# Loading the adjacency matrix in two halves from ScalarE's queue, and turning it by halves, in a two-layer graph network on one core

## The chip, the cores and the metric

The kernel runs on one core of one Trainium2 chip. The metric is the device time of one execution in microseconds; three executions of the kernel before gave 1511.56, 1512.70 and 1513.59, median 1512.7 us. A lower number is better.

## What is computed

The input `x` has 32 graphs of 512 nodes with 128 features, all in fp32, and `adj` is one 512 x 512 matrix shared by all. The reference, cut to what matters:

```python
# layer 0: graph convolution of order 3; both adjacencies are the same adj
parts = [x[..., None], chebyshev(adj, x), chebyshev(adj, x)]      # adj x, adj^2 x, adj^3 x, twice
x = layernorm(x + einsum('bnik,iok->bno', concat(parts, 3), weight_1))
# layer 1: five gated steps, then the residual
h = x
for _ in range(5):
    m = einsum('nm,bmd->bnd', adj, h); av = concat([m, m], -1)    # in and out matrix are both adj
    u = h @ u3.T + u3_b
    z = sigmoid(av @ w3.T + w3_b + u)
    r = sigmoid(av @ w4.T + w4_b + u)
    hv = tanh(av @ w5.T + w5_b + (r * h) @ u5.T + u5_b)
    h = (1 - z) * h + z * hv
x = layernorm(x + h)
```

Since the adjacency is the same throughout, the kernel adds the two halves of each layer-1 weight, and the weights of equal powers in layer 0. It computes layer 0 with the square of adj, which it forms once.

## The kernel before, in words

**Tiles and stages.** The 32 graphs go through as 16 pairs. `pair(q, key0)` describes one pair: `layer0`, then five steps, each made of a product of adj with both graphs' state (`pair_product`) and, for each graph, the gates (`gates`). The state is needed in two layouts: features on the partitions (`hT`) for the gates, nodes on the partitions (`X`) for the product with adj. Each step therefore ends with a turn of `hT` into `X`. From pair 2 on, layer 0 works on two pairs at once for the products with adj (`quad_product`).

**Products in seven.** Every product of 2 x 2 blocks is done with seven block products in place of eight (`seven`, line 393). The sums of blocks that this needs are made beforehand: `T` (four sums of adj's blocks, by VectorE, line 234), `TT` (the same one level down, line 249), `at2S` (sums of the square's blocks, line 496), and sums of the state's blocks `S` by POOL (line 511). In `seven`, products one, three, five and six go into one PSUM bank and are read out between by a copy on ScalarE (line 385) or an add on VectorE (lines 386, 389). Product three can't begin before the copy of product one, and so on.

**Turns.** By DMA, a turn is `turn` (line 345): VectorE turns 32 x 32 blocks into a buffer `v` (line 360), SP writes it to DRAM in four transfers and fetches it back in another order. There are five buffers `v`; layer 0 also takes two of them for its result (`vy`, line 857) and, for each turned input, one more as a landing place. By TensorE, a turn is four transposes (`transposes`, line 299) and a copy by ScalarE. `ON_PE = {14: 2, 15: 2}` (line 23) says how many last steps of which pair use TensorE (line 1073). Where the last step is among them, the end of the pair is not a turn either: `finish` (line 1010; `last_finish`, line 977, for the last pair) adds the residual and the turned state by products with the identity in PSUM, 4 + 4 for each graph (line 1018), and norms from there. Other pairs turn by DMA, add on POOL (line 1113) and norm from SBUF.

**The order of the work.** `Plan` (line 47) writes the order out by hand. Each operation has an engine, a cost in us, a key, the operations that it comes after, and the buffers that it takes and gives; `late` is how long after its issue a result counts as there (for a DMA, its latency). `run` (line 75) goes through time with these numbers and emits, on each free engine, the ready operation with the smallest key. The engines then execute exactly that order, each waiting on semaphores where something isn't there. `KEYS` (line 24) is the start key of each pair, `SQ_KEY` that of the square of adj, `TT_KEY` that of the sums `TT`.

**The opening.** SP issues the two graphs of pair 0 (`first_x`, line 218), then four transfers of a quarter of adj each (`load_adj`, line 213: blocks 11, 21, 12, 22; 256 KB each, 1 KB pieces), then layer 0's weight `w0` (line 257). ScalarE loads its table, and copies. TensorE turns pair 0's x (line 302), multiplies adj's blocks with x (line 524), and turns adj itself (`transposes` at line 434, four banks of four turns) for the left side of its square. ScalarE copies the four banks (`an`, line 437), VectorE sums their blocks (line 453), and the seven products of the square follow (line 460). The two graphs of pair 1 are loaded from ScalarE's queue (`second_x`, line 206), those of later pairs from SP's. `w0` is summed on VectorE into `wc` and `wt` (lines 261 to 267), the weights of layer 0's channel products (line 766).

The line that the new argument of the sums `T` replaces is 235; the waits of the pair's products on adj's blocks are at lines 550 and 551:

```python
T_sums.append(plan("DVE", 0.69, emit, after=at_in + T_sums[:2], key=-50.0))
...
(L[0], lambda: B11, [f11, in11]),
(L[1], lambda: B21, [f12, in21]),
```

Of the kernel before, what the change touches and what calls it, by code (L numbers as in the profile page):

```python
# [17 lines left out]
H = NK // 2  # L18
HN = N // 2
R = 32  # L20
NR = P // R
STEPS = 5
ON_PE = {14: 2, 15: 2}
KEYS = [-2.0, 20.0, 50.0, 68.0, 92.0, 118.0, 154.0, 168.0, 186.0, 214.0, 234.0, 268.0, 294.0, 322.0, 346.0, 358.0]
LONG = 19.0
TT_KEY = 45.0
SQ_KEY = 10.0
KEPT = 3
FIRST = 2
SINGLE = 2  # L30
# [96 lines left out]
def gnn_resnorm_kernel(  # L127
# [17 lines left out]
    nc = tc.nc  # L145
# [8 lines left out]
    def tiles(tag, n, shape=(P, N), pool=work):  # L154
        return [pool.tile(list(shape), F32, tag=f"{tag}_{i}", name=f"{tag}_{i}") for i in range(n)]

    slots = dict(
        bank=tiles("bank", 8, pool=psum),
# [7 lines left out]
        UY=tiles("UY", 2, (P, 4, N)),  # L166
        h0=tiles("h0", 4, (P, 2, NK, P)),
# [4 lines left out]
        z=tiles("z", 3),  # L172
        m=tiles("m", 5),
        S=tiles("S", 2, (P, 7, H, P)),
        v=tiles("v", 5),
        two=[None] * 5,
        inside=[None] * 17,
    )
    plan = Plan(slots)

    def chunk(k):
        return slice(k * P, (k + 1) * P)


    at = const.tile([P, NK, N], F32, tag="at", name="at")
    ident = const.tile([P, P], F32, tag="ident", name="ident")
# [23 lines left out]
        first = plan("ACT", 0.45, lambda: emit(0), after=after, key=-60.0, late=3.2)  # L210
        return first, plan("ACT", 0.45, lambda: emit(1), after=after, key=-60.0, late=3.2)

    def load_adj(i, j, key):
        k, c = slice(i * H, (i + 1) * H), slice(j * HN, (j + 1) * HN)
        emit = lambda: nc.sync.dma_start(at[:, k, c], adjT[:, k, c])
        return plan("SP", 0.46, emit, key=key, late=4.0)

    def first_x():
        emit = lambda: load_x(0, 0)
        a = plan("SP", 0.42, emit, take=[("xg", "xg0")], key=-99.0, late=2.9)  # L220
        b = plan("SP", 0.42, lambda: load_x(0, 1), key=-98.0, late=3.4)
        return a, b

    x_in = {0: first_x()}
    in11, in21 = load_adj(0, 0, -95.0), load_adj(1, 0, -94.0)
    at_in = [in11, in21, load_adj(0, 1, -90.0), load_adj(1, 1, -90.0)]

    B11, B12 = at[:, :H, :HN], at[:, :H, HN:]  # L230
    B21, B22 = at[:, H:, :HN], at[:, H:, HN:]
    T_sums = []
    for i, (a, b) in enumerate(((B12, B11), (B22, T[:, 0]), (B22, B12), (B21, T[:, 1]))):
        emit = lambda i=i, a=a, b=b: nc.vector.tensor_tensor(T[:, i], a, b, ALU.subtract)
        T_sums.append(plan("DVE", 0.69, emit, after=at_in + T_sums[:2], key=-50.0))


    TT_sums = []
    for i, n, of in (
# [8 lines left out]
        for j, (a, b) in enumerate(((b12, b11), (b22, t(0)), (b22, b12), (b21, t(1)))):  # L248
            emit = lambda d=t(j), a=a, b=b: nc.vector.tensor_tensor(d, a, b, ALU.subtract)
            after = T_sums + own[:2]  # L250
            own.append(plan("DVE", {4: 0.7, 2: 0.85, 1: 0.28}[n], emit, after=after, key=TT_KEY))
        TT_sums += own
# [1 line left out]


    w_of = lambda: plan["w0"].rearrange("p k f -> p (k f)")[:, : 7 * P]
    w0_in = plan("SP", 0.45, lambda: nc.sync.dma_start(w_of(), w0), take=[("UY", "w0")], key=-70.0, late=7.0)

    def layer0_weights():
        w_raw = w_of().rearrange("p (o k) -> p o k", k=7)  # L260
# [38 lines left out]
    def transposes(dst, src_of):  # L299

        for k in range(NK):
            nc.tensor.transpose(dst[:, chunk(k)], src_of(k), ident)  # L302
# [76 lines left out]
    def into(dst, cols, plus=None):  # L379

        def first(i, j):
            if plus is None:
                return "ACT", COPY[cols], lambda src: nc.scalar.copy(dst(i, j), src)  # L385
            return "DVE", ADD[cols], lambda src: nc.vector.tensor_tensor(dst(i, j), src, plus(i, j), ALU.add)

        def second(i, j):
            return "DVE", ADD[cols], lambda src: nc.vector.tensor_tensor(dst(i, j), src, dst(i, j), ALU.add)  # L389

        return first, second
# [39 lines left out]
    an_of = lambda km: plan[f"an{km // H}"].rearrange("p b k c -> p (b k c)").rearrange("p (k n) -> p k n", k=H)  # L431
    an_ready = []
    for km in range(NK):
        emit = lambda km=km: transposes(plan[f"ba{km}"], lambda k: at[:, k, chunk(km)])
        take = [("bank", f"ba{km}")] + ([("h0", f"an{km // H}")] if km % H == 0 else [])
        tr = plan("PE", 0.44, emit, after=at_in, take=take, key=SQ_KEY)
        emit = lambda km=km: nc.scalar.copy(an_of(km)[:, km % H], plan[f"ba{km}"])
        an_ready.append(plan("ACT", 0.59, emit, after=[tr], give=[("bank", f"ba{km}")], key=SQ_KEY))

    an_block = lambda i, l: lambda: an_of(l * H)[:, :, i * HN : (i + 1) * HN]  # L440
    an_sum = lambda i: lambda: plan[f"anS{i // H}"][:, i % H].rearrange("p k c -> p (k c)").rearrange(
# [3 lines left out]
    for i, (a, b, op) in enumerate(  # L445
# [7 lines left out]
        emit = lambda i=i, a=a, b=b, op=op: nc.vector.tensor_tensor(an_sum(i)(), a(), b(), op)  # L453
        take = [("h0", f"anS{i // H}")] if i % H == 0 else []
        sums.append(plan("DVE", 0.69, emit, after=an_ready + sums[-2:], take=take, key=SQ_KEY))

# [24 lines left out]
    give = [("h0", f"{t}{i}") for t in ("an", "anS") for i in range(2)]  # L481
    _, squared = seven("sq", an_ready, 1.72, terms, square_product, into(dst, N), SQ_KEY + 1, whole, give=give)

# [4 lines left out]
    for i, (a, b, op) in enumerate(  # L488
# [7 lines left out]
        emit = lambda i=i, a=a, b=b, op=op: nc.vector.tensor_tensor(at2S[:, i], a, b, op)  # L496
        A2_sums.append(plan("DVE", 0.69, emit, after=squared + A2_sums[-2:], key=SQ_KEY + 1))

    half_bank = lambda bank: bank[:, :HN]

    def copied(dst, src, turned, engine, after, key):

        to = nc.scalar.copy if engine == "ACT" else nc.gpsimd.tensor_copy
        emit = lambda: to(fit(dst(), turned), src())  # L504
        return plan(engine, 0.41 if engine == "ACT" else 0.4, emit, after=after, key=key)

    def fit(t, turned):
        return t.rearrange("p k (s d) -> p k s d", d=R) if turned else t

    def add(us, dst, a, b, op, after, key):  # L510
        emit = lambda: nc.gpsimd.tensor_tensor(dst(), a(), b(), op)  # L511
        return plan("POOL", us, emit, after=after, key=key)

    def pair_product(X_of, turned, name, dst, S, slots, after, key):

        X11, X12, X21, X22 = [
            lambda b=b, h=h: X_of(b)[:, h * H : (h + 1) * H] for b in range(2) for h in range(2)
        ]  # L520

        def product(dst, left, right, first, last):
            for k in range(H):
                nc.tensor.matmul(  # L524
                    dst,
                    lhsT=left[:, k, :],
                    rhs=right[:, k, :],
                    start=(first and k == 0),
                    stop=(last and k == H - 1),
                    skip_group_check=True,  # L530
                )

        own = plan("-", 0.0, lambda: None, after=list(after[0]), take=slots, key=key)
        both = list(after[1]) + [own]
        S_of = lambda i: lambda: S(i)
        F = lambda i: lambda: fit(S(i), turned)
        if turned:
            f11 = copied(S_of(4), X11, True, "ACT", [own], key)
            f12 = copied(S_of(5), X12, True, "ACT", [f11], key)
        else:  # L540
            f11 = f12 = own
        s0 = add(0.73, F(0), X21, X22, ALU.add, both, key)
        s1 = add(0.73, F(1), F(0), X11, ALU.subtract, [s0], key)
        s2 = add(0.73, F(2), X11, X21, ALU.subtract, both, key)
        s3 = add(0.73, F(3), X12, F(1), ALU.subtract, [s1], key)
        f22 = copied(S_of(6), X22, True, "POOL", both, key) if turned else own
        L = (S_of(4), S_of(5), S_of(6)) if turned else (X11, X12, X22)
        t = lambda i: lambda: T[:, i]
        terms = [
            (L[0], lambda: B11, [f11, in11]),  # L550
            (L[1], lambda: B21, [f12, in21]),
            (S_of(1), t(1), [s1, T_sums[1]]),
            (S_of(0), t(0), [s0, T_sums[0]]),
            (S_of(2), t(2), [s2, T_sums[2]]),
            (L[2], t(3), [f22, T_sums[3]] + both),
            (S_of(3), lambda: B22, [s3]),
        ]
        give = [o for o in slots if o[0] == "S"]
        p, (e11, e12, e21, e22) = seven(
            name, [f11], 0.86, terms, product, into(dst, HN), key, half_bank, give=give  # L560
        )
        read = [s0, s1, s2, s3, f11, f12, f22] if turned else p + [s2, s3]
        return [[e11, e12], [e21, e22]], [read] * 2
# [471 lines left out]
    def pair(q, key0):  # L1035
# [6 lines left out]
        for s in range(STEPS):  # L1042
# [27 lines left out]
            if s > 0:  # L1070
                for b in range(2):
                    plan("-", 0.0, lambda: None, after=read[b], give=[("X", f"X{q}_{s - 1}_{b}")], key=key)
            by_dma = s < STEPS - ON_PE.get(q, 0)

# [54 lines left out]
    for q in range(NP):  # L1129
        pair(q, KEYS[q])  # L1130
    with tc.manual_schedule(engines=None):
# [54 lines left out]
```

## Time and profile before

| What | Value |
|---|---|
| median of three executions | 1512.7 us |
| the profiled execution, its own time | 1512.07 us |
| its span, first to last instruction | 1510.3 us |
| TensorE busy | 1493.2 us, 99% of the span |
| VectorE, POOL, ScalarE busy | 1024.4, 848.7, 750.7 us |
| adj's four transfers, issue to landing | 5.0 to 5.6 us |
| pair 0's x, first half, issue and first use | 0.72 and 3.69 us |
| w0, issue and landing | 3.63 us and 6.1 us later |

The profile is of one execution. "PE" is TensorE's matmul, "PEld" its weight load, DVE VectorE, ACT ScalarE, POOL GpSimd; an engine's name with q is its sequencer, which issues DMAs. A list of instructions in order of time shows start and length in us, engine, line, operation, output and input tiles with their shape, the count, and in brackets the idle time before it with what ended it. A matmul's length includes its drain, so following matmuls overlap. The chain of work goes back from the last instruction to what released each one. A list of waits shows who waited for whom: total us, times, longest.

### The profile page before, as it was taken

The numbers are of one execution on the slowest core, as the hardware profiler recorded it, in microseconds if no ns is written. First come the engines' busy times: TensorE is split into PE (matmuls) and PEld (weight loads), VectorE is DVE, ScalarE is ACT, GpSimd is POOL, SyncE is SP. The second block draws the span as 40 slices with busy tenths as digits, with TensorE's granted clock in tenths as the row PEclk, the third lists the DMA queues.
The fourth block names the chain that finished last, engine by engine and source line by source line (L and its number), as shares of the span: only waits on it lengthen the run. The fifth ranks groups of instructions, "written<-read, shape, count | busy, mean of one in ns | idle before, by whom it ended". The sixth has DMA issues, their size and how long they took to land.

```text
span 1510.3 us, 21064 instructions
## 1 busy us (share of the span) xinstructions
PE 1493.2 (99%) x6562; PEld 1042.3 (69%) x6562; DVE 1024.4 (68%) x2125; ACT 750.7 (50%) x1584; POOL 848.7 (56%) x1207
## 2 busy tenths in 40 slices
PE   8999999999999999999999999999999999999997
PEld 7877777676667776677676766676766776666665
DVE  6566666767776758667767567768477666766665
ACT  3454444654644644455445445546444455545454
POOL 4856834764544947756367455558464644543454
PEclk9999999999999999999999999999999999999998
DMA  3114423333333433334243242534333332433310
GB/s 110 57 56 112 107 75 92 110 107 84 105 103 107 126 98 93 107 95 119 71 139 90 77 120 92 133 98 126 81 109 92 90 84 70 119 86 89 77 50 28
DMA packets 166176, 142.91 MB, mean 95 GB/s; under 512 B 18992, under 2 KB 128048, under 8 KB 166064
## 3 DMA queue, kind: packets, MB, share of 16 engines
q1 hardware_dynamic: 165776, 141.04, 33.9%
q8 instruction: 52, 0.85, 0.3%
q14 instruction: 60, 0.49, 0.1%
q10 hardware_dynamic: 288, 0.52, 0.1%
HBM read 71.76 MB, written 69.73 MB: 94 GB/s over the span
## 4 chain that ended last, share of the span: by engine, by line
PE 94%; DVE 2%; POOL 1%; issue 1%; DMA 1%; SPq 0%; ACT 0%; POOLq 0%; DVEq 0%
PE bank L909 35%; PE bank L524 32%; PE bank L1049 9%; PE bank L766 6%; PE bank L831 6%; PE bank L628 4%; PE bank L460 1%; PE bank L302 0%; POOL rstd L320 0%; POOL S L511 0%; DVE M L685 0%; DMA at<-in_adjT 0%; DVE UY L685 0%; PE bank L1018 0%; DMA X<-d 0%
## 5 line engine op out<-in xcount | busy, mean ns | idle before, releaser
L974 POOL TENSOR_TENSOR hT<-z,hT 128x512 f32<-128x512 f32 x156 | 199.0, 1281 | 303.9 <-DVE z L972 297.9
L524 PE MATMUL bank<-T,S 128*128 128x256 f32 x1232 | 307.0, 379 | 0.2 <-POOL S L511 0.2
L524 PEld LDWEIGHTS bank<-T,S 128*128 128x128 f32 x1232 | 229.1, 190 | 78.2 <-ACT m L385 28.9
L385 ACT COPY m<-bank 128x256 f32<-128x256 f32 x320 | 119.1, 372 | 277.6 <-PE bank L524 276.5
L524 PE MATMUL bank<-at,S 128*128 128x256 f32 x824 | 211.4, 379 | 0.9 <-ACT S L504 0.6
L389 DVE TENSOR_TENSOR m<-bank,m 128x256 f32<-128x256 f32 x240 | 100.3, 419 | 137.0 <-PE bank L524 94.7
L524 PEld LDWEIGHTS bank<-at,S 128*128 128x128 f32 x824 | 153.7, 190 | 57.3 <-issue 37.3
L970 DVE TENSOR_TENSOR bank<-bank,hT 128x512 f32<-128x512 f32 x156 | 107.8, 694 | 104.4 <-ACT bank L956 103.6
L909 PE MATMUL bank<-rh,u5s 128*128 128x512 f32 (+1 forms) x324 | 159.3, 587 | 0.2 <-ACT bank L936 0.2
L1049 PE MATMUL bank<-hT,u3s 128*128 128x512 f32 x320 | 159.3, 592 | 0.0
L909 PE MATMUL bank<-m,w4s 128*128 128x512 f32 x320 | 158.6, 592 | 0.0
L909 PE MATMUL bank<-m,w3s 128*128 128x512 f32 x320 | 157.0, 592 | 0.0
L909 PE MATMUL bank<-m,w5s 128*128 128x512 f32 x320 | 155.1, 593 | 0.2 <-DVE M L389 0.2
L917 ACT ACTIVATE bank<-bank 128x512 f32<-128x512 f32 x160 | 93.2, 583 | 121.1 <-DVE bank L915 120.7
L1054 ACT ACTIVATE uT<-bank,ub3s 128x512 f32<-128x512 f32 x160 | 109.7, 687 | 83.9 <-PE bank L1049 82.7
L915 DVE SCALAR_TENSOR_TENSOR bank<-bank,b4s,uT 128x512 f32<-128x512 f32 x160 | 119.6, 750 | 46.3 <-PE bank L909 44.1
L956 ACT ACTIVATE bank<-bank,hv_b 128x512 f32<-128x512 f32 x158 | 104.3, 662 | 77.1 <-PE bank L909 76.0
L922 DVE SCALAR_TENSOR_TENSOR bank<-bank,b3s,uT 128x512 f32<-128x512 f32 x160 | 118.9, 750 | 13.8 <-PE bank L909 13.1
L924 ACT ACTIVATE z<-bank 128x512 f32<-128x512 f32 x160 | 95.1, 595 | 59.9 <-DVE bank L922 55.7
L360 DVE STREAM_TRANSPOSE v<-hT 128x512 f32<-128x512 f32 x152 | 105.5, 699 | 20.0 <-POOL hT L974 19.4
L918 DVE TENSOR_TENSOR rh<-bank,hT 128x512 f32<-128x512 f32 x160 | 107.8, 679 | 10.0 <-ACT bank L917 9.2
L972 DVE TENSOR_TENSOR z<-bank,z 128x512 f32<-128x512 f32 x156 | 105.1, 682 | 1.6
(182 smaller groups left out, 2456.1 us busy)
## 6 DMA issues: line engine op xcount, KB each, us to landing
d<-v SPq DMA_DIRECT2D x832, 64.0 KB, 1.8
X<-d SPq DMA_DIRECT2D x152, 256.0 KB, 2.8
v<-d SPq DMA_DIRECT2D x56, 256.0 KB, 2.8
xg<-in_x SPq DMA_DIRECT2D x30, 256.0 KB, 3.0
out<-h SPq DMA_DIRECT2D x30, 256.0 KB, 2.1
hd<-h SPq DMA_DIRECT2D x13, 512.0 KB, 3.8
h<-hd SPq DMA_DIRECT2D x13, 512.0 KB, 3.9
at<-in_adjT SPq DMA_DIRECT2D x4, 256.0 KB, 5.3
```

The source lines that it names most:

```text
L360: blocks = lambda: nc.vector.transpose(plan[f"v{name}"], src_of())
L385: return "ACT", COPY[cols], lambda src: nc.scalar.copy(dst(i, j), src)
L524: nc.tensor.matmul(dst, lhsT=left[:, k, :], rhs=right[:, k, :], start=(first and k == 0), stop=(last and k == H - 1), skip_group_check=True,)
L909: nc.tensor.matmul(plan[dst][:, c], lhsT=w, rhs=plan[src][:, c], start=first, stop=last, skip_group_check=True)
L915: emit = lambda: nc.vector.scalar_tensor_tensor(plan[pr], plan[pr], b4s, plan[uT], ALU.add, ALU.add)
L918: emit = lambda: nc.vector.tensor_tensor(plan[rh], plan[pr], plan[h], ALU.mult)
L922: emit = lambda: nc.vector.scalar_tensor_tensor(plan[pz], plan[pz], b3s, plan[uT], ALU.add, ALU.add)
L970: emit = lambda: nc.vector.tensor_tensor(plan[ph], plan[ph], plan[h], ALU.subtract)
L972: emit = lambda: nc.vector.tensor_tensor(plan[z], plan[ph], plan[z], ALU.mult)
L974: emit = lambda: nc.gpsimd.tensor_tensor(plan[h], plan[z], plan[h], ALU.add)
L1049: emit = lambda bn=bn, hb=h[b]: nc.tensor.matmul(plan[bn], lhsT=u3s, rhs=plan[hb], start=True, stop=True)
L1054: emit = lambda bn=bn, uT=uT: nc.scalar.activation(plan[uT], plan[bn], AF.Identity, bias=ub3s)
```

## The change

Adj is loaded by two transfers, each with two of the four rows of blocks (512 KB, 4 KB pieces), issued by ScalarE as its first instructions, while SP issues the two halves of x. `w0` is issued by ScalarE after x is there. The sums `T` wait only for the half that they use. The turns of adj are emitted by halves, two transposes at a time, so that those of the first half don't wait for the second. The latencies that the plan counts with are 5.0 and 6.6 us for adj and 6.0 for w0. Besides: `ON_PE` gives one step to each of pairs 13 and 14 and two to pair 15, the keys are others, there are four buffers `v`, and `inside`, of which each pair takes one, has 18 entries.

```diff
-ON_PE = {14: 2, 15: 2}
-KEYS = [-2.0, 20.0, 50.0, 68.0, 92.0, 118.0, 154.0, 168.0, 186.0, 214.0, 234.0, 268.0, 294.0, 322.0, 346.0, 358.0]
+ON_PE = {13: 1, 14: 1, 15: 2}
+KEYS = [-8.0, 12.0, 42.0, 60.0, 84.0, 110.0, 146.0, 166.0, 178.0, 208.0, 228.0, 260.0, 294.0, 322.0, 342.0, 354.0]
-TT_KEY = 45.0
-SQ_KEY = 10.0
+TT_KEY = 36.0
+SQ_KEY = 4.0
...
-        v=tiles("v", 5),
+        v=tiles("v", 4),
-        inside=[None] * 17,
+        inside=[None] * 18,
...
-    def load_adj(i, j, key):
-        k, c = slice(i * H, (i + 1) * H), slice(j * HN, (j + 1) * HN)
-        emit = lambda: nc.sync.dma_start(at[:, k, c], adjT[:, k, c])
-        return plan("SP", 0.46, emit, key=key, late=4.0)
+    def load_adj(i, late):
+        k = slice(i * H, (i + 1) * H)
+        return plan("ACT", 0.45, lambda: nc.scalar.dma_start(at[:, k], adjT[:, k]), key=-95.0 + i, late=late)
...
-    in11, in21 = load_adj(0, 0, -95.0), load_adj(1, 0, -94.0)
-    at_in = [in11, in21, load_adj(0, 1, -90.0), load_adj(1, 1, -90.0)]
+    at_in = [load_adj(0, 5.0), load_adj(1, 6.6)]
...
-        T_sums.append(plan("DVE", 0.69, emit, after=at_in + T_sums[:2], key=-50.0))
+        T_sums.append(plan("DVE", 0.69, emit, after=at_in[: 1 + min(i, 1)] + T_sums[:2], key=-50.0))
...
-    w0_in = plan("SP", 0.45, lambda: nc.sync.dma_start(w_of(), w0), take=[("UY", "w0")], key=-70.0, late=7.0)
+    w0_in = plan("ACT", 0.45, lambda: nc.scalar.dma_start(w_of(), w0), after=x_in[0], take=[("UY", "w0")], key=-70.0, late=6.0)
...
-        emit = lambda km=km: transposes(plan[f"ba{km}"], lambda k: at[:, k, chunk(km)])
-        take = [("bank", f"ba{km}")] + ([("h0", f"an{km // H}")] if km % H == 0 else [])
-        tr = plan("PE", 0.44, emit, after=at_in, take=take, key=SQ_KEY)
+        tr = []
+        for half in range(2):
+
+            def emit(km=km, half=half):
+                for k in range(half * H, (half + 1) * H):
+                    nc.tensor.transpose(plan[f"ba{km}"][:, chunk(k)], at[:, k, chunk(km)], ident)
+
+            take = [("bank", f"ba{km}")] + ([("h0", f"an{km // H}")] if km % H == 0 else [])
+            take = take if half == 0 else []
+            tr.append(plan("PE", 0.22, emit, after=[at_in[half]] + tr, take=take, key=SQ_KEY))
         emit = lambda km=km: nc.scalar.copy(an_of(km)[:, km % H], plan[f"ba{km}"])
-        an_ready.append(plan("ACT", 0.59, emit, after=[tr], give=[("bank", f"ba{km}")], key=SQ_KEY))
+        an_ready.append(plan("ACT", 0.59, emit, after=tr, give=[("bank", f"ba{km}")], key=SQ_KEY))
...
-            (L[0], lambda: B11, [f11, in11]),
-            (L[1], lambda: B21, [f12, in21]),
+            (L[0], lambda: B11, [f11, at_in[0]]),
+            (L[1], lambda: B21, [f12, at_in[1]]),
```

Lines of the kernel after stand two lower than the kernel before's from about line 300 on and five higher from line 500 on (turns by TensorE of x and hT at 300, copies at 383, products of adj at 529, gates at 914, `finish` at 1023).

## The prediction

> **What bounds the kernel now.** I read the page's busy times first, then TensorE's waits, then the opening and the tail as lists of instructions and as the chain of work.
>
> ```profile
> span 1510.3 us, 21064 instructions
> PE 1493.2 (99%) x6562; PEld 1042.3 (69%) x6562; DVE 1024.4 (68%) x2125; ACT 750.7 (50%) x1584; POOL 848.7 (56%) x1207
> ```
>
> TensorE is the bound: 99% busy, the next engine 68%. A busy share counts a matmul's drain, so I price TensorE's work by the distance from one matmul to the next. The chain of work gives it (start, length, what):
>
> ```profile
> 1453.30 0.44 PE bank L302 x4
> ...
> 1471.40 6.01 PE bank L909 x14
> ...
> 1478.27 0.89 PE bank L1018 x8
> 1479.16 2.59 PE bank L524 x12
> 1481.76 1.78 PE bank L1018 x16
> ```
>
> Division gives 0.111 us for 128 columns (0.89/8), 0.216 for 256 (2.59/12), 0.429 for 512 (6.01/14). A turn (L302) is one instruction, every other fp32 product two. The program's order holds 64 turns and 1271 + 1180 + 798 products of 128, 256 and 512 columns: 64 x 0.1108 + 2 x (1271 x 0.1108 + 1180 x 0.2163 + 798 x 0.4293) = 1484.4 us. So 1510.3 - 1484.4 = 25.9 us of the span are not TensorE's work at full rate; only these can be won. Where they lie:
>
> ```profile
> PE bank L302 <- DMA xg<-in_x: 3.7, 1, 3.7
> PE bank L986 <- POOL hT L950: 2.2, 1, 2.2
> PE bank L524 <- DMA at<-in_adjT: 1.0, 1, 1.0
> PE bank L766 <- POOL S L511: 0.9, 2, 0.8
> ```
>
> (us in total, times, longest.) And the opening, in order of time:
>
> ```profile
> 1.63 1.96 SPq L215 DMA_DIRECT2D at<-in_adjT  x4
> ...
> 3.69 1.94 PE L302 MATMUL bank<-ident,xg 128*128 128x128 f32 x8 [3.69 <-DMA xg<-in_x]
> ...
> 6.64 3.78 PE L524 MATMUL bank<-at,xg 128*128 128x256 f32 x8 [1.02 <-DMA at<-in_adjT]
> ...
> 10.74 1.03 PE L524 MATMUL bank<-T,S 128*128 128x256 f32 x4
> ```
>
> The first 8 turns and 8 products take 0.22 and 0.43 us each, twice what they take later. Up to the next instruction at 10.22, work worth 8 x 0.111 + 8 x 0.216 = 2.6 us was done: 7.6 us are lost in the opening. The tail: the last pair's gates begin at 1489.5 with 9.5 us of TensorE work left and 20.8 us to go, so 11.3 are lost. The remaining 7.0 lie between, in waits of 1.0 us and less; from 1200 to 1480 TensorE shows no idle time at all.
>
> **The Trainium skill.** "TensorE: Matmul & The Clock Gate", Part 1: the array runs at half rate until it has been busy for about 3.4 us, counted in windows that run freely. The trace agrees: half rate from 6.64 to about 10.2, 3.6 us after work became continuous; the earlier 1.9 us of turns, followed by the 1.0 us wait, had not sufficed. "DMA: Bandwidth & Descriptors", Queues, rings and completion order: each DMA engine alternates between the queues that have work. Its Rules for kernel authors add that spreading transfers over issuing engines saves issue time and no bandwidth. The trace agrees on bandwidth: from 2.5 to 7.5 us the DMA engines are 80 to 100% busy and more, at 260 to 417 GB/s. It shows no two queues at once in the opening.
>
> **The change, part by part.**
>
> *adj from ScalarE's queue in halves.* Removed from SP: four issues (1.96 us together) and w0's (0.47). ScalarE issues two (0.44 each by its L198 rows) ahead of its table load (1.28); that then ends near 2.9, and its first copy is due at 4.81: 1.9 us of cover, cost nothing. The issue of adj moves from 1.63 to 0.72, but 0.5 MB of x and 1.05 MB of adj share engines that are full. Half one of adj (0.52 MB) now alternates with x (0.52 MB). The measured flow has moved 1.05 MB at about 5.4 us; landing was about 0.7 to 1 after the last byte (x's first: 0.26 MB moved by 2.9, landed 3.65). So half one lands near 5.9 (5.2 to 6.6, the old landing as worst), half two near 7.5. x's first part, no longer alone, lands near 4.1 in place of 3.65. The second part follows near 4.8; eight turns at half rate end near 5.9. The first product starts at 6.0, not 6.64: 0.6 us won, and continuous work, hence full rate, starts 0.6 us earlier too if the window falls alike. The price: TensorE's idle time before its first turn grows by 0.4, but those turns were followed by a wait anyway.
>
> *w0 on ScalarE.* Its issue (0.45) delays only the second copy of x. It lands near 10; VectorE reads it at 13.4 today. 3 us of cover: nothing. SP's next transfers wait for a buffer until 10.51, so freeing SP wins nothing.
>
> *adj's turns by halves, products among them.* 16 turns before and after. In the new order the turns and the first pair's products alternate, so no product waits for half two before about 8.5. Against that, ScalarE now issues the second pair's x (2 x 0.44) and copies one turned block (0.59) before the third product's copy. I count product three ending near 11.8, copy to 12.4, issues and turned copy to 13.9, copy of product five to 14.3: product six, ready near 14.0, waits 0.35. The second pair's x, issued 12.4 and landing 3.0 later, is wanted by TensorE at 15.2: another 0.2. Squares of adj need all four turned blocks, copied by about 16.5 against 14.6 before; second-pair work inserted ahead (0.44 + 0.87 us and the first pair's seventh product) covers that. Of 0.6 to 1.2 us won, 0.3 remains by 18 us. Bounds: -1.0 (window of the clock falls badly, x late) to +2.0.
>
> *ON_PE.* Pair 13 gets its last step through TensorE (`finish`): 2 x (4 + 4) products of two instructions, 32 x 0.111 = 3.55 us, as the 0.89 + 1.78 + 0.89 of L1018 show for pair 14. Pair 14 loses the turns of one step: 8 x 0.111 = 0.89. Net +2.65 us on the bound; the whole new order sums to 1487.0 against 1484.4. It lands where TensorE has no idle time to hide it, and its counterpart, fewer DMA turns and POOL sums near the end, relieves engines that nothing waits for there. Paid in full.
>
> *KEYS, TT_KEY, SQ_KEY, one v buffer fewer, `inside` 18.* No instruction added. `inside` has 17 slots for 16 pairs: nothing. The keys reorder everything after the opening. The wait at 54 us stays: the chain from the y product through VectorE's moments and POOL's powers (48.4 to 55.5) is still covered by the same eleven products of 0.44 us. From w4 to u5 of one gate both orders leave at least 3.9 us of other work for a chain of about 2.5. I take 0 for the middle's 7.0 us and keep -3 to +5.
>
> *Tail.* The last step has the same instructions. Before, one normalising step (L330, 0.47) sits between the last two activations of z (L924, L943) on the closing path; in the new order it doesn't: -0.5 (0 to -0.5).
>
> Sum: 1512.07 (the profiled execution's own time, 1.8 above its span) + 2.65 - 0.3 - 0.5 + 0 = 1513.9. The median shown is 0.6 above that execution, so 1514.5, +0.12%.
>
> **The rivals.** I call within 0.2% (1509.7 to 1515.7) no change; about what can be told of this kernel.
>
> *Forecast, chance 0.56:* 1514.5, own range 1512.3 to 1516.5. Extra work paid, small gain in the opening.
>
> *Four v buffers hold up the turns (slower), 0.20.* A turn holds a v for about 0.7 + 1.8 + 1.8 = 4.3 us; layer 0 takes two for its y and, for turned nodes, two more. With five, one remained for a running pair's turn; with four none does at that moment, and X comes later. Price: up to 4.3 us for each of 14 later pairs, as far as the other pairs in flight don't cover it. It decides once more than a tenth is uncovered: 14 x 0.43 = 6. Time: 1514.5 + 4 = 1518.5. For it: VectorE and SP stand in a fixed order, so one late v holds up what is behind. Against: waits before TensorE for DMA in the middle are nil now.
>
> *The opening and the middle give more (faster), 0.14.* adj in by 5.2 and full rate by 8: 2 us; two of the 7.0 us between vanish with the new keys; tail 0.5: 1512.7 + 2.65 - 4.5 = 1510.9. For it: the middle has that much to give. Against: the wait at 54 us has the same cover.
>
> *adj does not come earlier, 0.10.* The DMA engines were full and x now shares them; first product at 6.6 or later, window of the clock missed: gain -1. Time: 1512.7 + 2.65 + 1.0 - 0.5 = 1515.9.
>
> **How the numbers follow.** Slower by over 0.2%: a sixth of the forecast's cases (0.09), nearly all of the v case (0.19), over half of the last (0.06), and with an order remade throughout, some more for stalls I can't see: 0.38. Faster by over 0.2% needs 3 us beyond paying 2.65: half of the third case, 0.08. Same: 0.54. Range 1510.8 to 1519: from the faster case's time to just above the v case's.
>
> **What would show it.** Right: L529 with at and xg starts near 6.0 with no wait over 0.3 before it; the landing of at near 5.2 from issue for half one; 32 more instructions of the `finish` row (L1023), 8 fewer turns with hT; TensorE's idle time elsewhere unchanged, wait near 54 us kept. Wrong: TensorE waits in the middle by DMA of X or by S, more than 5 us in sum; v's transposes on VectorE waiting for SP; a first product before 5.2; a tail from the last w4 to the end other than 20 to 21 us.

## The result, and the profile after

The changed kernel took 1517.3 us (median of eight executions, 1515.6 to 1518.9); the kernel before took 1511.7 us beside it (eight, 1510.0 to 1513.6). The ratio is 1.0036, 95% interval 1.0025 to 1.0047: slower by 5.4 us. The prediction was 1514.5 us with a range of 1510.8 to 1519.0. The time lies in the range but outside the range of the main forecast (1512.3 to 1516.5): the sum was about 3 us short, and the experiments are about where these 3 us are.

From the page of the changed kernel's profile, the span and the busy times:

```profile
span 1515.9 us, 21141 instructions
PE 1495.7 (99%) x6586; PEld 1046.0 (69%) x6586; DVE 1022.1 (67%) x2125; ACT 748.5 (49%) x1586; POOL 844.8 (56%) x1206
```

TensorE is still the bound. It has the 24 instructions more (6586 for 6562) that ON_PE was to add, and is busy 2.5 us longer. The span grew by 5.6, so less than half of the loss is added work. TensorE's waits in the changed kernel (us in total, times, longest):

```profile
PE bank L300 <- DMA xg<-in_x: 6.4, 2, 6.1
PE bank L991 <- POOL hT L955: 1.9, 1, 1.9
PE bank L771 <- DVE UY L387: 1.6, 1, 1.6
PE bank L529 <- POOL S L516: 0.7, 1, 0.7
```

The largest differences from before: the wait for x was 3.7 us and is 6.4. The wait for adj (1.0) is gone, and in its place stands a wait of 1.6 us for UY, a sum by VectorE, which the kernel before did not have. The last wait of the kernel (for hT from GpSimd) fell from 2.2 to 1.9. The waits for S hardly changed: 0.7 and 0.5, for 0.9 and 0.2. The opening of the changed kernel in order of time:

```profile
0.72 0.89 ACTq L215 DMA_DIRECT2D at<-in_adjT  x2
...
6.05 1.08 PE L300 MATMUL bank<-ident,xg 128*128 128x128 f32 x4 [6.05 <-DMA xg<-in_x]
...
7.47 1.11 PE L300 MATMUL bank<-ident,xg 128*128 128x128 f32 x4 [0.33 <-DMA xg<-in_x]
...
8.38 1.91 PE L529 MATMUL bank<-at,xg 128*128 128x256 f32 x4
...
10.51 1.39 PE L529 MATMUL bank<-T,S 128*128 128x256 f32 x4
```

adj is issued at 0.72 as planned, and its first half is there at 6.14, where VectorE first reads it. But x, also issued at 0.72, turns at 6.05 instead of 3.69, and the first product starts at 8.38 instead of 6.64. The transfer that was moved forward came within its predicted 5.2 to 6.6 us; it was the transfer beside it that came late.

The table splits each profiled execution by where TensorE stands still: the start of its first turn, then the idle time between its matmuls in each stretch (the gaps that the lists in order of time show; a matmul is taken to leave the array 0.16 us, its drain, before its recorded end). The ratios are of all executions, the idle times of one. The mean granted clock of a profile (0.995 to 0.998 here) doesn't say how fast it was: it counts stretches at half rate in the opening and the tail, where TensorE waits much of the time, and e6 has both the lowest clock (0.995) and the shortest span (1509.4 us). In e9 and e16 there is a half-rate stretch in the middle too, which the idle times don't count; it is treated there.

| kernel | ratio to the kernel before, 95% | first turn | idle to 22 us | 22 to 75 | 75 to 1480 | after 1480 |
|---|---|---|---|---|---|---|
| before | 1 | 3.69 | 1.2 | 1.5 | 3.2 | 2.7 |
| after | 1.0036 [1.0025, 1.0047] | 6.05 | 0.7 | 3.7 | 2.6 | 2.8 |
| e1 adj behind x on SP | 1.0038 [1.0026, 1.0051] | 3.86 | 3.7 | 3.9 | 1.4 | 2.8 |
| e2 old ON_PE | 1.0015 [1.0007, 1.0023] | 6.13 | 0.9 | 3.8 | 1.9 | 2.2 |
| e3 five v | 1.0038 [1.0025, 1.0050] | 5.74 | 1.8 | 3.9 | 2.4 | 2.8 |
| e4 before with new ON_PE | 1.0026 [1.0016, 1.0037] | 3.64 | 0.9 | 1.5 | 4.5 | 1.7 |
| e6 before with less ON_PE | 1.0014 [1.0007, 1.0021] | 3.67 | 0.5 | 1.5 | 3.6 | 6.6 |
| e8 adj 0.2 us later | 1.0033 [1.0021, 1.0046] | 3.91 | 2.5 | 3.8 | 2.3 | 2.8 |
| e9 TT sums held back | 1.0048 [1.0035, 1.0061] | 6.19 | 0.9 | 4.1 | 0.6 | 2.8 |
| e10 opening alone | 1.0040 [1.0028, 1.0053] | 5.76 | 1.4 | 3.9 | 2.9 | 2.7 |
| e11 1 KB pieces | 1.0021 [1.0012, 1.0031] | 4.25 | 1.4 | 3.3 | 1.2 | 2.8 |
| e12 turns whole | 1.0048 [1.0034, 1.0061] | 6.08 | 0.4 | 3.8 | 3.1 | 2.8 |
| e14 1 KB pieces, old ON_PE | 1.0005 [0.9997, 1.0013] | 4.23 | 1.1 | 3.2 | 2.2 | 2.2 |
| e16 as e14, turns first | 1.0026 [1.0017, 1.0034] | 4.20 | 1.5 | 4.4 | 2.2 | 2.2 |

Read by row, the change costs three things: added work (no column; 32 instructions more and 8 fewer), a start of TensorE 2.4 us later, and 2.2 us of new idle time between 22 and 75 us.

### The profile page after: what moved, and what is told of

The parts are those of the page before. It is cut to its first block, busy times and chain, and to the rows that moved or that the text cites. A ratio compares the mean times of both kernels' runs of the same rounds, so it can differ in the third digit from the quotient of the medians.

```text
span 1515.9 us, 21141 instructions
## 1 busy us (share of the span) xinstructions
PE 1495.7 (99%) x6586; PEld 1046.0 (69%) x6586; DVE 1022.1 (67%) x2125; ACT 748.5 (49%) x1586; POOL 844.8 (56%) x1206
## 4 chain that ended last, share of the span: by engine, by line
PE 96%; DVE 1%; POOL 1%; issue 1%; DMA 1%; ACT 0%; SPq 0%; POOLq 0%; DVEq 0%; ACTq 0%
PE bank L914 36%; PE bank L529 32%; PE bank L1054 9%; PE bank L836 6%; PE bank L771 6%; PE bank L633 5%; PE bank L1023 0%; DMA xg<-in_x 0%; DVE TT L247 0%; PE bank L465 0%; POOL S L516 0%; PE bank L300 0%; DVE h L458 0%; POOL rstd L318 0%; DMA d<-v 0%
## 5 line engine op out<-in xcount | busy, mean ns | idle before, releaser
L979 POOL TENSOR_TENSOR hT<-z,hT 128x512 f32<-128x512 f32 x154 | 195.0, 1272 | 307.2 <-DVE z L977 295.8
```

The costliest lines, as they stand in the source:

```text
L979: emit = lambda: nc.gpsimd.tensor_tensor(plan[h], plan[z], plan[h], ALU.add)
```

## The experiments

**The opening: who starves x?** First theory: x shares the DMA engines with adj, and it is enough to put x ahead. Rival: halves of 512 KB are the trouble in any place.

> The kernel after, except that SP issues adj's two halves right behind the two of x, in place of ScalarE beside them; every engine's order of work stays. Theory: in the kernel after, x is starved by adj on the other queue, landing at 6.0 and 7.4 us in place of 3.6 and 4.2, and this and VectorE's backlog that follows (a wait of 1.6 us before TensorE at 29 us) are the part of the loss that the forecast missed. Then the first turn starts at 3.7 us again, the first product near 6.8, the wait at 29 us shrinks below 0.6, and the time falls by 2 to 4 us against the kernel after, to 1513.5 to 1515.5. Rival: the opening is set by adj's half of 512 KB, not by x; then x lands early and TensorE waits for adj instead, first product at 8 or later, time within 1 us of the kernel after (1516.5 to 1518).

```diff
-        return plan("ACT", 0.45, lambda: nc.scalar.dma_start(at[:, k], adjT[:, k]), key=-95.0 + i, late=late)
+        emit = lambda: nc.sync.dma_start(at[:, k], adjT[:, k])
...
+        emit_b = lambda: [load_x(0, 1), behind_x[0]()]
```

Measured: 1518.3 us, ratio 1.0038. x is back at 3.86, and the time did not fall. TensorE's waits of this kernel:

```profile
PE bank L307 <- DMA xg<-in_x: 3.9, 1, 3.9
PE bank L536 <- DMA at<-in_adjT: 3.1, 1, 3.1
```

What was the wait for x is now a wait for adj's first half: it is first used 7.3 us after its issue (quarters in the kernel before landed after 5.0 to 5.6 us), and the first product starts at 8.93. Between 4.0 and 5.5 us the DMA engines moved 202 GB/s here and 296 in the kernel before, with one queue at work in both. The kernel before moves adj in pieces of 1 KB (in a quarter, 256 fp32 numbers lie together), this one and the changed kernel in pieces of 4 KB (1024 numbers). But the changed kernel, with x's queue beside the 4 KB pieces, moved 309 GB/s in the same stretch, so the pieces alone don't make the slow flow; why it is slow here stays open. The theory that x's late arrival alone is the cause fell, and the size of the pieces became the next suspect.

> The kernel after with one tiny copy on ScalarE ahead of adj's issues, so that its table load (1.28 us) comes first and adj is issued from ScalarE's queue near 2.3 us, when x is mostly under way; order of the rest unchanged. Theory (x starved by sharing the engines, not by the queue as such): x lands below 4.7 us, half one of adj near 7, time 1 to 3 us below the kernel after, 1514.5 to 1516.5. Rival (a second queue delays x whenever it is issued, or adj's landing is what counts): x still lands at 5.5 or later, or the first product starts later than 8.4; time as the kernel after or above.

```diff
+        def emit():
+            if i == 0:
+                nc.scalar.copy(lead, mhalf)
+            nc.scalar.dma_start(at[:, k], adjT[:, k])
```

A tiny copy ahead of adj's issue puts ScalarE's table load first, so that x has a lead. The trace gives adj's issue at 0.90 only, but its packets begin later than that tells: by 3.0 us two packets of adj had begun (18 in the changed kernel) and 0.24 MB of x (0.07). Measured: 1517.3 us, 1.0033, as the changed kernel. The first part of x turned at 3.91, the second at 7.05, after a wait of 2.1 us (0.33 in the changed kernel), and the first product started at 7.96. A lead brings x's first part early beside 4 KB pieces too, and hands the delay to the second.

> The kernel after with each half of adj issued as two transfers of 1 KB pieces (four of 256 KB) from ScalarE's queue, still beside x; 26 of TensorE's rows move. Theory: the DMA engines take turns between the two queues piece by piece or packet by packet, so x with 2 KB pieces gets a larger share against 1 KB pieces than against 4 KB ones: x's first part lands at 4.0 to 5.0 us in place of 6.0, the first product starts near 7.2, and the time falls by 0.5 to 2 us, to 1515.3 to 1516.8. Rival: the share goes by bytes or the engines' order of start, not by piece; then x still lands near 6 and the time is that of the kernel after within 0.7.

```diff
+        def emit():
+            for j in range(2):
+                c = slice(j * HN, (j + 1) * HN)
+                nc.scalar.dma_start(at[:, k, c], adjT[:, k, c])
```

Same queue, same place, but each half as two transfers with pieces of 1 KB. Measured: 1514.3 us, 1.0021, 2.3 us better than the changed kernel by the ratios. Its opening:

```profile
4.25 1.09 PE L305 MATMUL bank<-ident,xg 128*128 128x128 f32 x4 [4.25 <-DMA xg<-in_x]
5.92 1.12 PE L305 MATMUL bank<-ident,xg 128*128 128x128 f32 x4 [0.59 <-DMA xg<-in_x]
6.83 1.91 PE L534 MATMUL bank<-at,xg 128*128 128x256 f32 x4
```

x turns 1.8 us earlier than in the changed kernel, and the first product starts 1.55 us earlier, at 6.83. How the DMA engines were shared shows two differences. A row gives the queue (q1 is SP's with x, q10 ScalarE's with adj), its packets, MB, and its share of the 16 engines. The changed kernel, from 1.5 to 3.0 us and from 3.0 to 5.5:

```profile
q1 hardware_dynamic: 35, 0.07, 54.2%
q10 hardware_dynamic: 18, 0.07, 22.4%
...
q10 hardware_dynamic: 134, 0.49, 56.5%
q1 hardware_dynamic: 153, 0.28, 34.3%
```

and the kernel with 1 KB pieces:

```profile
q1 hardware_dynamic: 67, 0.14, 79.5%
...
q10 hardware_dynamic: 436, 0.43, 54.5%
q1 hardware_dynamic: 220, 0.39, 42.2%
```

First, in the kernel with 1 KB pieces adj's packets begin later: none by 3.0 us, though its issue is at 0.72 in both, and x has the engines to itself till then. Second, once both queues move, x gets 0.28 of 0.77 MB beside 4 KB pieces and 0.39 of 0.82 MB beside 1 KB pieces. The trace counts a piece as a packet (x's are 2 KB). One of x's passed for about one of adj's with 4 KB pieces, but for about two of adj's with 1 KB pieces, so a turn by single pieces fits only the first. The Trainium skill, "DMA: Bandwidth & Descriptors", Queues, rings and completion order, has each DMA engine go round its queues packet by packet, and its packet is a bundle of descriptors. Such a larger turn fits both: a transfer of x has 128 pieces, and one of adj has 128 of 4 KB in the changed kernel and 256 of 1 KB here. That is argued from the counts, not shown, since the edit halves each transfer as well as cutting its pieces. Nor do the runs separate the later start from the larger share; e8 shows that a lead alone can bring the first part this early.

**The added work.**

> The kernel after with ON_PE as before ({14: 2, 15: 2}); TensorE's order differs only in its last 80 rows or so. Theory: the 2.65 us of TensorE work that the new ON_PE adds are paid in full, so the time falls by 2.2 to 3.1 us, to 1514.2 to 1515.1. Rival: the end of pair 13 by DMA lengthens the tail and gives the work back; time within 1 us of the kernel after.

```diff
-ON_PE = {13: 1, 14: 1, 15: 2}
+ON_PE = {14: 2, 15: 2}
```

Measured: 1514.1 us, 1.0015. Taking ON_PE's change back wins 0.0021 of the time, 3.2 us.

> The kernel before with the new ON_PE alone. If the work that ON_PE moves to TensorE is paid in full, +2.65 us over the kernel before: 1514.4, ratio 1.0017. If part of it fell into waits of the end (2.7 us of gaps there), less than +1.3: below 1513.0. If the change's numbers for ON_PE only work with its new keys, more than +4.

The same line changed the other way in the kernel before. Measured: 1515.6 us, 1.0026, that is 3.9 us slower, interval 2.4 to 5.6. Its idle time by the end fell (1.7 us after 1480, for 2.7) and rose in the middle (4.5 for 3.2). A third estimate comes from e11 and e14 (the latter below): 1.0021 - 1.0005, 2.4 us. All three hold 2.65 within their spread; the work is paid in full.

> The kernel before with ON_PE = {15: 2}: pair 14 too ends by DMA turn and POOL, 4.4 us of TensorE work less (32 products of 0.111 and 8 turns of 0.111). Theory (near the end TensorE's work is paid in full, in both directions): 3 to 4.4 us below the kernel before, near 1508. Rival: that work fills time in which the last pair's chain keeps TensorE waiting anyway, or pair 14's end by DMA becomes the last; then within 1.5 us of the kernel before or above it.

```diff
-ON_PE = {14: 2, 15: 2}
+ON_PE = {15: 2}
```

The kernel before with 4.4 us less work on TensorE. Measured: 1513.7 us, 1.0014: slower, not faster, though its profiled execution was its quickest (1511.3). TensorE's waits of that execution show where the saving goes:

```profile
PE bank L302 <- DMA xg<-in_x: 3.7, 1, 3.7
PE bank L986 <- POOL hT L950: 3.7, 1, 3.7
PE bank L524 <- ACT m L385: 1.4, 3, 0.5
PE bank L986 <- DVE hT L950: 1.3, 1, 1.3
```

With pair 14's turns gone from TensorE there is less to do while the last hT is made: the wait for it grows from 2.2 to 3.7 + 1.3, and idle time after 1480 us from 2.7 to 6.6. The clock that TensorE was granted from 1498 to 1502 us was 0.50 as well, and 1.00 in the kernel before. So of the three settings tried, the old ON_PE is the best: work beyond it is paid, work short of it comes back as waiting. What makes the other executions slower still than the profiled one isn't shown.

**The rival of four v buffers.**

> The kernel after with five v buffers as before; the order of work changes in some 290 of TensorE's 1936 rows. Theory (the v buffers cost nothing; the waits after 75 us sum to about 3 us in both kernels): time within 1.5 us of the kernel after, 1515.8 to 1518.8. Rival (four v buffers hold up the turns): 3 us or more below, 1514.3 or less.

```diff
-        v=tiles("v", 4),
+        v=tiles("v", 5),
```

Measured: 1518.1 us, 1.0038, no difference from the changed kernel. The v rival, which had a chance of 0.20 and a price of 4 us, fell. It would have looked right by the time alone.

**The new wait near 30 us.** In the changed kernel in order of time:

```profile
27.14 1.22 DVE L247 TENSOR_TENSOR TT<-T,TT 128x512 f32<-128x512 f32 x1
...
28.28 0.94 DVE L247 TENSOR_TENSOR TT<-at 128x256 f32<-128x256 f32 x1
...
30.22 0.41 DVE L387 TENSOR_TENSOR UY<-bank,UY 128x256 f32<-128x256 f32 x1
...
30.77 0.68 PE L771 MATMUL bank<-wc,S 128*128 128x128 f32 x4 [1.59 <-DVE UY L387]
```

TensorE waits for a bank that VectorE has yet to add into UY, and this sum stands behind four sums of TT in VectorE's fixed order. VectorE's groups from 16 to 32 us (times, then busy us and mean ns), kernel before:

```profile
L453 DVE TENSOR_TENSOR h<-h,h 128x512 f32<-128x512 f32 x3 | 2.8, 921 | 0.0
...
L249 DVE TENSOR_TENSOR TT<-T,TT 128x512 f32<-128x512 f32 x2 | 1.4, 676 | 0.0
```

and changed kernel:

```profile
L458 DVE TENSOR_TENSOR h<-h,h 128x512 f32<-128x512 f32 x3 | 3.7, 1218 | 1.2 <-ACT h L442 1.2
L247 DVE TENSOR_TENSOR TT<-T,TT 128x512 f32<-128x512 f32 x2 | 2.4, 1218 | 0.0
```

The same five sums take 6.1 us instead of 4.2, and VectorE first stands still for 1.2 us, waiting for h, which comes later. A sum of 512 columns takes 0.68 us when GpSimd is idle (at 25.61 in the changed kernel) and up to 1.24 beside GpSimd's sums of S; here all five fall beside them. The Trainium skill, "SBUF — State Buffer", SBUF: two separate sides, says that a VectorE operation with two SBUF inputs and a GpSimd operation that reads SBUF exclude each other for the whole instruction. The lengths agree with that: GpSimd's sums of 256 columns also take 0.72 to 1.18 us here. No run keeps the two engines apart to test it.

So VectorE runs later and slower. Which part of the change does it? The next kernels each take a candidate away.

> The kernel after with the twelve sums TT held back in the plan until its time 34 us (TensorE first uses them near 78 us), so that VectorE doesn't make them between 13 and 31 us; 43 of TensorE's rows move. Theory: after the later opening VectorE is full from 20 to 30 us, and the TT sums stand ahead of the adds that TensorE waits for at 24 and 29 us (0.2 to 0.6 and 1.4 to 1.8 us of idle time, in the kernel after and in the three before this). Then these waits vanish, idle time from 22 to 75 us falls from 3.7 to 3.9 us to about 2, and the time falls by 1.5 to 2.5 us against the kernel after, to 1514.8 to 1515.9. Rival: those adds are late because of the PSUM copies and POOL ahead of them, not TT; then the wait stays and the time is within 0.8 us of the kernel after, 1516.5 to 1518.

```diff
+    quiet = plan("-", 0.0, lambda: None, key=-99.0, late=34.0)
...
-            after = T_sums + own[:2]
+            after = T_sums + own[:2] + [quiet]
```

With TT's sums held back the wait near 30 us is gone, but the idle time from 22 to 75 us is 4.1 us; it stands at 55 to 61 us instead, where the kernel waits 1.1 us for GpSimd's S and 1.0 for ScalarE's UY. 1518.6 us, 1.0048: no gain. Its profile shows a further cost, in the clock. A row gives the stretch, its length, the busy time of PE, PEld, DVE, ACT and POOL, then the granted clock, the DMA share and GB/s:

```profile
60.00:62.00 2.00, 1.35 (x6) 1.35 (x7) 0.09 (x1) 1.87 (x5) 2.00 (x4) 0.60 0.01 4
62.00:64.00 2.00, 2.00 (x8) 1.73 (x7) 0.95 (x2) 0.98 (x2) 2.00 (x4) 0.54 0.06 16
64.00:66.00 2.00, 2.00 (x16) 1.92 (x16) 0.42 (x1) 0.81 (x2) 2.00 (x4) 1.00 0.51 118
```

The clock is at half for 3.4 us from 60.4, towards the end of these waits, which is about 1.7 us of work lost; the changed kernel has 1.00 there. From 75 to 1480 us this execution idles 2.0 us less than the changed kernel. So a gain was there, and new waits and the half rate took it back; for the other executions of e9 no trace is kept.

> The opening of the kernel after alone: adj in two halves and w0 from ScalarE, sums T and turns of adj by halves; ON_PE, all keys and five v buffers as before. TensorE's order is that of before except for some 50 rows in the first 50 us. Theory: the opening costs 1.5 us until the first square and 2 more through VectorE's backlog, and the keys and v cost nothing: 3 to 4 us above the kernel before (1512.2 beside the last runs), 1515.2 to 1516.2 in its terms. Rival one, only the first 20 us count: 1.2 to 1.8 above. Rival two, the loss is in the keys or the v buffers: within 0.8 of the kernel before.

The kernel with the change's opening, and ON_PE, KEYS, TT_KEY, SQ_KEY and the v buffers of the kernel before:

```diff
-ON_PE = {13: 1, 14: 1, 15: 2}
+ON_PE = {14: 2, 15: 2}
...
-SQ_KEY = 4.0
+SQ_KEY = 10.0
...
-        v=tiles("v", 4),
+        v=tiles("v", 5),
```

1516.6 us, 1.0040, about 6.0 us above the kernel before, where 3 to 4 were expected. The wait for UY stays (1.2 us) and 3.9 us are idle between 22 and 75, so neither the keys nor ON_PE make it: the opening does. It is also slower than e2, which has the new keys (1.0015), and the intervals don't touch. The new keys win about 3.8 us with this opening, by the ratios (the four v buffers, which e2 also has, made no difference in e3). The two profiled executions differ by 1.8 us only; by the table 1.0 us of it lies between 75 and 1480, 0.5 in the tail and 0.5 before 22 us, less 0.4 for a later first turn.

> The changed kernel with adj's turns whole again: all four turns of a bank stand together behind both halves, as in the kernel before; everything else of the change stays. If the turns by halves are what costs time between 22 and 75 us (they stand two by two among the products, the first copy to h ends 4 us later than before, and VectorE's sums of h and TT then queue beside GpSimd's), the copies to h come earlier, the wait of 1.6 us for VectorE's UY near 30 us goes or shrinks below 0.5, and the time falls by about 1.5 us from the changed kernel's 1517.3, to 1515.8, a ratio of about 1.0027 to the kernel before. If VectorE is late for any order of the turns, because its sums beside GpSimd take 1.2 us instead of 0.7, a wait of the same size stands at another place and the time stays at 1517.3 (1.0036).

```diff
-            tr.append(plan("PE", 0.22, emit, after=[at_in[half]] + tr, take=take, key=SQ_KEY))
+        tr = plan("PE", 0.44, emit, after=at_in, take=take, key=SQ_KEY)
```

1518.3 us, 1.0048. The wait for UY is 1.7 us and the idle time in that stretch 3.8. Turning adj by halves was not the cause.

> The changed kernel with 1 KB pieces (each half of adj as two transfers) and the old ON_PE. The small pieces alone gave 1514.3 and the old ON_PE alone took 3.2 us off the changed kernel. If the two causes are separate and add, this gives 1514.3 - 3.2 to 1514.3 - 2.65 = 1511.1 to 1511.6, the kernel before within 0.1%, and the change's opening is then worth about what was predicted (-0.3) once its pieces are small. If the small pieces gain only because the longer tail hides something, or the old ON_PE gains only behind a late opening, they don't add: 1512.8 or more.

The two edits of e11 and e2 together: 1513.0 us, 1.0005 [0.9997, 1.0013], not to be told from the kernel before. By ratio, 1.0036 less 0.0021 for ON_PE and 0.0015 for the pieces is 1.0000, which the interval holds, so the two about add. The time itself lies on the other side of the line drawn beforehand (1512.8), so it doesn't prove it. 3.2 us are still idle between 22 and 75.

> The changed kernel with 1 KB pieces, the old ON_PE and, in addition, SQ_KEY at -12: adj's turns stand first on TensorE, ahead of the first products with x, as soon as a half is there. No work is added. It stands against 1 KB pieces with the old ON_PE (1513.0, with 3.2 us lost between 22 and 75 us, 1.5 in the kernel before). If the lost time in the middle comes from the products that an early adj lets run ahead of the turns, so that the copies to h, and VectorE's sums of h behind them, come later than in the kernel before, the copies come some 2 us earlier here, the wait for VectorE's UY (1.1 us) goes, and the time falls by 1.0 to 1.7: 1511.3 to 1512.0, the kernel before or a little less. If VectorE simply has too much to do in the first 30 us for a TensorE that starts earlier, a wait of the same size stands at another place: 1513.0 within 0.5, or more when x's eviction comes later.

```diff
-SQ_KEY = 4.0
+SQ_KEY = -12.0
```

On top of e14, adj's turns stand ahead of the products. The four copies to h were done by 14.4 us instead of 17.1, and the wait for UY by VectorE went, as the theory had it, but 1516.3 us were measured, 1.0026, 3.2 us more than e14 by the ratios. TensorE's new wait in that kernel:

```profile
PE bank L776 <- POOL S L521: 2.1, 1, 2.1
```

It ends at 57 us. GpSimd's sum of xT and uT begins at 24.80 here and at 16.64 in e14, since the copy uT that it needs follows a product that stands behind 32 instructions of adj's square; the order that brings h forward puts GpSimd back. Here too the granted clock is at half for 3.4 us, from 59.5 (0.50 from 60 to 62 us), about 1.7 us of work; with the 1.6 us by which the table's idle times up to 75 us exceed e14's, that comes to about the 3.2. So the theory that an early adj lets the products run ahead of the turns got its first half right, the wait for VectorE, but the edit moves another engine's work as well, and no gain came of it.

No kernel here beats the kernel before: e14 comes nearest.

## Why the prediction was right and wrong, by its steps

*adj from ScalarE's queue in halves (predicted 0.6 us won on the first product): wrong, and the step that failed.* Half one was predicted to land near 5.9 and came by 6.14. But the step took the alternation of the two queues as about an equal share of bytes, and put x at 4.1 and 4.8. x got 0.28 of 0.77 MB from 3.0 to 5.5 us, and its two parts turned at 6.05 and 7.47. The first product started at 8.38, not at 6.0. In e11, with transfers of 256 KB in 1 KB pieces, the share is about equal (0.39 of 0.82 MB) and the first turn at 4.25, close to the 4.1 of the prediction. The first product is then at 6.83 and not at 6.0, because x's second part still comes late (turns at 5.92) and adj's first half, in small pieces, is first read at 6.80.

*Opening as a whole: -0.3 predicted, +1.5 measured.* At the first product of adj with h TensorE has lost 9.2 us in the changed kernel (at 19.18) and 7.7 in the kernel before (at 14.65): the time, less the work done up to there at the prediction's prices per product. The first turn 2.4 us later costs that much; 0.9 comes back, in part because the first product no longer waits 1.0 us for adj. The lower bound of the step was "-1.0 (window of the clock falls badly, x late)", a loss of 1.0, and the loss was outside it.

*w0 on ScalarE (nothing): as far as seen, right.* Issued at 7.18, landed 3.3 us later, read at 14.37.

*ON_PE (+2.65, paid in full): right.* 24 instructions more on TensorE, 2.5 us more of busy time, and 2.4, 3.2 and 3.9 us in three pairs of kernels. The cheaper direction doesn't exist either (e6), which the prediction did not ask.

*Keys and the middle (0, kept from -3 to +5): the size was off.* Counted like the opening, TensorE loses 2.5 us more between 22 and 75 us and 0.35 less from 75 to 1480: +2.15. (Time less priced work at 22, 75 and 1480 us and at the end: 7.7, 9.8, 14.6 and 25.9 before, 9.2, 13.8, 18.3 and 28.8 after. The idle times of the table give +1.6; they leave out what is lost in gaps too short to be listed.) The prediction looked for waits by DMA of X and for v, and TensorE's list has none by DMA in the middle. What came was a bank that VectorE had not emptied; "no instruction added" was true of VectorE and of no help, since five sums grew by 1.9 us by standing beside GpSimd's. The wait near 54 us that was to stay did stay (0.53 us for S at 59.47).

*Tail (-0.5): right.* From the last w4 to the end it was 20.8 us and is 20.1 (1495.78 to 1515.9). The normalising step is gone from between the last two activations of z: they start 0.48 us apart, and 0.82 before.

Together: 1.5 + 2.65 + 2.15 - 0.7 = 5.6, the growth of the span. Against the prediction's sum, 1.8 us come from the opening and 2.15 from the middle.

*By the parts of the change, with luck.* The stretches of time hide what each part did, since the opening acts into the middle. The kernels take the parts in turn, by the ratios to the kernel before: the opening alone costs 6.0 us (e10; interval 4.2 to 8.0), the new keys with four v buffers take 3.8 off that (e10 to e2), and the new ON_PE puts 3.2 back (e2 to the changed kernel): 5.4. The prediction had -0.3, -0.5 (0 for the keys and -0.5 for the tail) and +2.65. So it was off by some 6 us in the opening and by some 3 the other way in the keys, and its range held because the two partly cancel: with the opening and ON_PE alone the estimate would be 1511.7 + 9.2 = 1520.9, above the range. What the new keys do without this opening was not run.

*The rivals.* "adj does not come earlier" had the right place and the wrong transfer. It expected 1515.9, with 1.0 us lost by x and adj sharing full engines. Adj did come earlier and x paid; of all the cases this one was nearest in mechanism, at a chance of 0.10. The v case was nearest by time (1518.5) and wrong by e3. The gain from the keys that the case of a faster kernel saw did happen, 3.8 us with this opening, and the opening overpaid it.

*Left open.* Why TensorE idles 2 us more between 22 and 75 us. The opening brings it: every kernel with it has 3.2 to 4.4, every kernel without it 1.5. Not ON_PE, the keys, the v buffers, the late x, TT's sums or the turns by halves alone, each of which was taken away while it stayed. That VectorE's and GpSimd's sums now fall together is what the lists show, but as a cause it is only argued: where one wait was removed, others of the same size stood in its place. Two parts of the opening were not tried alone: w0 on ScalarE's queue, and the differences of T that start on half of adj and now run beside GpSimd's first sums (1.22 and 1.21 us for two of them; all four took 0.68 to 0.69 before).

## What to carry to other kernels

Before giving a transfer its own queue, ask which transfer it will run beside and how large the two and their contiguous pieces are: here a queue with transfers of 512 KB in 4 KB pieces took nearly two thirds of the bytes from one with 256 KB in 2 KB pieces, and the starved one was what the first instruction waited for. Where a bound engine is 99% busy, added work was a sure cost here and an earlier start only a possible gain, so the sure term should set the expectation; less work was no sure gain (e6), since the last chain then had less to hide behind. When the engines' orders are fixed, a delay of two microseconds in the opening can stay as a wait that moves from place to place; taking the named wait away is no proof of its cause until the total falls. A forecast that comes out near its number should still be checked part by part, since two parts can be wrong in opposite directions.

## What the runs showed of the hardware that was not expected

- Two queues at once: x's first 256 KB in 2 KB pieces, always issued at 0.72, turned at 6.05 us beside adj's 512 KB transfers in 4 KB pieces, at 4.25 beside 256 KB transfers in 1 KB pieces, and at 3.69 and 3.86 with adj behind it on the same queue.
- While both queues moved (3.0 to 5.5 us), one piece of x passed for about one of adj's 4 KB pieces (153 to 134 packets) and for about two of its 1 KB pieces (220 to 436).
- One queue alone: with 4 KB pieces of adj behind x the DMA engines moved 202 GB/s from 4.0 to 5.5 us, with 1 KB pieces 296. Larger pieces were not faster there.
- VectorE's sum of 512 fp32 columns: 0.68 us, up to 1.24 beside GpSimd's.
- In e9 and e16 TensorE's clock fell to half for 3.4 us in mid-kernel, at the end of waits of 2.1 and 3.4 us in sum within 5 us; in the changed kernel, with 0.75 us of waits there, it did not.
